# Adaptive-norm attention followed by a GRU: projections split around the transposes, and a last attention batch reordered by pairs of heads

## The chip, the cores and the metric

The kernel runs on one core of one Trainium2 chip. The metric is the device time of one execution in microseconds (us), the median of several executions on one chip. Five engines are spoken of by their profile names: PE (TensorE; its weight loads are listed apart as PEld), DVE (VectorE), ACT (ScalarE), POOL (GpSimd) and SP, whose queue issues nearly all DMAs. All arithmetic is float32.

## The reference

Sixteen sequences (B = 16) of T = 256 tokens with D = 512 features go through an attention block and then a GRU, each with a residual.

```python
# attention, 16 heads of 32
xn  = rms_norm(x, g_norm) * (1 + scale) + shift      # scale, shift from cond @ W_emb + b_emb
q, k, v = split(xn @ W_qkv)
q, k = rms_norm(q, g_q), rms_norm(k, g_k)            # per head
o   = softmax(q @ k.T * 32 ** -0.5) @ v
x   = x + o + o @ W_out
# GRU over the 256 tokens, all 16 sequences at once, state h (16 x 512), h0 = cond
for t in range(256):
    gi, gh = x[:, t] @ W_ih + b_ih, h @ W_hh + b_hh
    r, z = sigmoid(gi_r + gh_r), sigmoid(gi_z + gh_z)
    n = tanh(gi_n + r * gh_n)
    h = (1 - z) * n + z * h
    out[:, t] = x[:, t] + h
```

## The kernel before

The program has two parts: attention, batch by batch, up to about 620 us, and the GRU, step by step, after that. Within each part the order on PE, DVE, ACT and POOL is the order in which the program text issues the instructions; nothing is reordered later. Only SP's DMAs are placed by the framework.

**Attention.** A batch has 16 heads, taken as four groups of four. For a group, `logits` (line 302) multiplies q by k into four PSUM banks `lg0` to `lg3`, one for each head; the contraction is over 32 features, so the four heads use four bands of 32 rows of the array. `maxima` (L326, DVE) takes the negated row maxima, `exps` (L330, ACT) the exponentials with their row sums, `normalize` (L340: a reciprocal on DVE, eight scalings on POOL) divides. In the next group's time the normalised weights are transposed on PE (`turn`, in two halves by `turn_pair`, L350), copied from PSUM into `attnT` (`put_turned_bank`, L371, two banks by DVE and two by ACT), multiplied with v (`weigh`, L383), and the result is copied to `oT` (`put_weighed`, L399).

One group is one slot. PE's spare places in the slots of batch b are filled with the projections of batch b + 1: `project` (L238) adds, for each chunk `k` of 128 features, four matmuls (j = 0 to 3) of 128 x 32 weights against 512 columns. The four write four bands of 32 PSUM partitions, that is four bands of 32 columns of the array. `slot0` to `slot3` (L418 to L538) write out by hand what goes where:

- slot 0: eight chunk steps of `project` for q and k, with `turn_x` (transposes of x) and the turn of the previous group among them;
- slots 1 and 2: five chunk steps ahead of the turn and one behind it, then `weigh`;
- slot 3: four ahead, then the transposes of q and k of one half (`turn_qk`), the turn, `turn_qk` of the other half, two chunk steps, `weigh`.

In slot 3 `turn_qk` needs the normalised q and k that DVE makes in `norm_qk` (L269).

Fifteen batches go through these slots. The sixteenth has no next batch to project; `last_batch` (L586) takes its four groups alone. There a loop pass transposes the previous group in two halves, runs the maxima and exponentials of the current one, copies the transposed banks, and issues the logits of the next group for all four heads; `weigh` of a group comes a pass later. Behind the loop stand the four parts of `project_first` (L545: output projection of the first 16 tokens, 32 matmul records each), the work on the last group, and `open_gates` (L567), which writes the biases into the PSUM banks of the first gates.

**GRU.** W_hh is loaded into `whh`, in the same SBUF place as `wq`, once the last projection has read that. Step 0 begins with three `state_part` calls on the initial state, `h0P`, one for each gate (L881), then `input_part` for two steps. The first instruction of the recurrence proper is the DVE transpose `trr` of gate r (L831).

Of the kernel before, what the change touches and what calls it, by code (L numbers as in the profile page):

```python
# [8 lines left out]
F32 = mybir.dt.float32  # L9
AF = mybir.ActivationFunctionType  # L10
ALU = mybir.AluOpType
AX = mybir.AxisListType
PSUM = bass.MemoryType.PSUM

P = 128
# [4 lines left out]
def kernel(  # L20
# [214 lines left out]
            else:  # L235
                nc.vector.tensor_scalar(dst, tps[r][:, c], a, s, ALU.mult, ALU.add)  # L236

    def project(b, n, s, ks, a):  # L238

        if isinstance(a, str):  # L240
            a = tile_ps(f"qkv_{b}_{n}_{s}", a)
        for k in ks:
            for j in range(4):
                nc.tensor.matmul(  # L244
                    a[32 * j : 32 * j + 32, :],
                    batches[b].xnT[:, k, n * P + 32 * j : n * P + 32 * j + 32],
                    wq[:, k, s * D : (s + 1) * D],
                    start=(k == 0),
                    stop=(k == KC - 1),
                )  # L250
        return a
# [47 lines left out]
    class Group:  # L299
        pass  # L300

    def logits(b, g):

        w = Group()
        w.b, w.g = b, g
        w.lg = [
            ps_lg.tile([P, NT, T], F32, tag=f"lg{i}", name=f"lg_{b}_{g}_{i}") for i in range(HG)
        ]
        for n in range(NT):
            for i in range(HG):  # L310
                r = slice(i * DH, (i + 1) * DH)
                nc.tensor.matmul(  # L312
                    w.lg[i][:, n, :],
                    qT[r, g, n * P : (n + 1) * P],
                    kT[r, g, :],
                    start=True,
                    stop=True,
                )
        w.turned = []
        w.neg = small.tile([P, HG, NT], F32, tag="neg", name=f"neg_{b}_{g}")  # L320
        w.den = small.tile([P, HG, NT], F32, tag="den", name=f"den_{b}_{g}")
        w.rden = small.tile([P, HG, NT], F32, tag="rden", name=f"rden_{b}_{g}")
        w.attn = [None] * HG
        return w

    def maxima(w, heads):  # L326
        for i in heads:
# [131 lines left out]
    def slot1(b, w, prev, st):  # L459
        m = b + 1  # L460
        project(m, 0, 1, (2, 3), st.k)
        st.q1 = project(m, 1, 0, (0, 1, 2), "Z")
        maxima(w, range(HG))
        exps(w, range(HG))
        sq = st.s0.square(1, st.k)
        turn(prev)
        put_turned(prev, "vava")
        project(m, 1, 0, (3,), st.q1)
        st.s0.add(1, sq)
        if b + 3 < B:  # L470
            norm_first(b + 3, (0,))
        st.s0.rs.first()
        st.s1 = Stats(m, 1)
        st.sq = st.s1.square(0, st.q1)
        weigh(prev, "Y")
        put_weighed(prev)
        st.rstd = st.s0.rs.second()
        normalize(w)

    def slot2(b, w, prev, st):  # L480
        m = b + 1
        k = project(m, 1, 1, range(KC), "Y")
        maxima(w, range(HG))
        st.qk0 = norm_qk(m, 0, (st.q, st.k), st.rstd)
        st.v0 = project(m, 0, 2, (0,), "A")
        exps(w, range(HG))
        st.s1.add(0, st.sq)
        sq = st.s1.square(1, k)
        turn(prev)
        put_turned(prev, "vava")  # L490
        project(m, 0, 2, (1,), st.v0)
        st.s1.add(1, sq)
        if b + 3 < B:
            norm_first(b + 3, (1,))
        st.s1.rs.first()
        if b + 3 < B:
            batches[b + 3].rs.first()
        weigh(prev, "X")
        put_weighed(prev)
        if b == 0:  # L500

            for c in range(KC):
                d = wo[:, c, c * P : (c + 1) * P]
                nc.vector.tensor_tensor(d, d, ident, ALU.add)
            load_small()
        elif b == 2:
            for i in range(2):
                a = b_rows[:, 2 * i, :]
                nc.vector.tensor_tensor(a, a, b_more[:, i, :], ALU.add)
        st.accs = (st.q1, k)  # L510
        st.rstd = st.s1.rs.second()
        normalize(w)

    def slot3(b, w, prev, st):
        m = b + 1
        project(m, 0, 2, (2, 3), st.v0)
        st.v1 = project(m, 1, 2, (0, 1), "X")
        maxima(w, range(HG))
        qk1 = norm_qk(m, 1, st.accs, st.rstd)
        tq0 = turn_qk(m, 0, st.qk0, "ZY")  # L520
        if b + 3 < B:
            rstd = batches[b + 3].rs.second()
        exps(w, range(HG))
        put_qk(0, 0, tq0, nc.vector)
        put_qk(0, 1, tq0, nc.scalar)
        put_v(m, 0, st.v0)
        turn(prev)
        put_turned(prev, "vava")
        tq1 = turn_qk(m, 1, qk1, "ZY")
        project(m, 1, 2, (2, 3), st.v1)  # L530
        put_qk(1, 0, tq1, nc.vector)
        put_qk(1, 1, tq1, nc.scalar)
        if b + 3 < B:
            norm_apply(b + 3, rstd)
        normalize(w)
        weigh(prev, "A")
        put_weighed(prev)
        if m == B - 1:  # L538
            put_v(m, 1, st.v1)
# [27 lines left out]
    def open_gates(p, which=(R_, N_, Z_)):  # L567

        for g, name, bank, row, n in (
# [6 lines left out]
            for j in range(4):  # L576
# [6 lines left out]
                    skip_group_check=True,  # L583
                )

    def last_batch(prev):  # L586


        b, before = B - 1, None
        w = logits(b, 0)  # L590
        for g in range(NG):
            if before:
                weigh(before, "Z")
            turn_pair(prev, 0, "AX")
            maxima(w, (0, 1))
            exps(w, (0, 1))
            if before:
                put_weighed(before, nc.vector)
            turn_pair(prev, 1, "YZ")
            maxima(w, (2, 3))  # L600
            exps(w, (2, 3))
            put_turned_bank(prev, 0, nc.vector)
            normalize(w, (0, 1))
            put_turned_bank(prev, 2, nc.vector)
            put_turned_bank(prev, 1, nc.scalar)
            put_turned_bank(prev, 3, nc.scalar)
            if g < NG - 1:
                normalize(w, (2, 3))
                before, prev, w = prev, w, logits(b, g + 1)
        project_first(0)  # L610
        project_first(1)
        normalize(w, (2,), nc.vector)
        normalize(w, (3,))
        turn_pair(w, 0, ("lg2", "lg3"))
        turn_pair(w, 1, "AX")
        weigh(prev, "Z")
        put_turned(w, "vava")
        put_weighed(prev)
        open_gates(0, (R_, N_))
        weigh(w, "Y")  # L620
        put_weighed(w, nc.vector)
        open_gates(0, (Z_,))
        project_first(2)
        project_first(3)

    E = mybir.EngineType
    E = mybir.EngineType
    ORDERED = {E.PE, E.DVE, E.Activation, E.Pool}
    with tc.manual_schedule(engines=ORDERED):
# [5 lines left out]

        pe = tile_ps("ps_emb", "Z", (P, 8 * 32))
        nc.vector.memset(pe, 0.0)

        warm = tile_ps("warm", "Y", (P, P))
        for i in range(12):  # L640
            nc.tensor.matmul(warm, ident, ident, start=True, stop=True)
        tp = tile_ps("tp_h0", "X", (P, KC, B))
        nc.tensor.transpose(
            tp.rearrange("p k b -> p (k b)"), cond_sb, ident[: KC * B, : KC * B]
# [72 lines left out]
        for b in range(B - 1):  # L717
            for g in range(NG):
                w = logits(b, g)
                (slot0, slot1, slot2, slot3)[g](b, w, prev, st)  # L720
                prev = w
        last_batch(prev)

    TG = P // B
    xins = {}

    def in_blocks(a, i, j, s):

        a = a[:, i * TG : (i + 1) * TG, :].rearrange("b (s i) (j f) -> s j b i f", s=2, f=P)
        return a[s, j]

    def load_block(i):
        if i < T // TG:
            xins[i] = xin.tile([P, TG // 2, KC, 32], F32, tag="xin", name=f"xin_{i}")
            for j in range(4):
                for s in range(2):
                    r = 32 * j + B * s
                    nc.sync.dma_start(  # L740
                        xins[i][r : r + B].rearrange("b i q c -> b i (q c)"), in_blocks(x, i, j, s)
                    )

    for i in range(4):
        load_block(i)


    whh = wpool.tile([P, KC, 3 * D], F32, tag="w_b", name="whh")
    load_rows(whh, w_hh)

    work.close()

# [49 lines left out]
        nc.scalar.copy(gates[N_, p % 2][:, 0, :], b_rows[:, 3, :])  # L802
        nc.scalar.copy(gates[Z_, p % 2][:, 0, :], b_rows[:, 2, :])

    def gate_part(dst, rows, w, first, k, stationary):

        for j in range(4):
            nc.tensor.matmul(  # L808
                dst[32 * j : 32 * j + rows],
                stationary,  # L810
                w[:, k, :].rearrange("p (g j c) -> p j g c", g=3, c=P)[:, j, first::2][:, : dst.shape[1]],
                start=False,
                stop=True,
                skip_group_check=True,
            )

    def input_part(p, g, k):

        grp, ti = divmod(2 * p, TI)
        x2 = xTs[grp][:, k, ti : ti + 2, :].rearrange("p t b -> p (t b)")  # L820
        gate_part(gates[g, p % 2], 32, wih, g, k, x2)

    def state_part(t, g, hT):

        for k in range(KC):
            gate_part(gates[g, t // 2 % 2][:, 0:1, :], hT.shape[2], whh, g, k, hT[:, k, :])

    def turned(name, t, gate):

# [39 lines left out]
    with tc.manual_schedule(engines=ORDERED):  # L869
# [7 lines left out]
        for c in (slice(0, 2 * B), slice(2 * B, TI * B)):  # L877
            for i, o in enumerate(first):
                a = xTs[0][:, 2 * i : 2 * i + 2].rearrange("p q t b -> p q (t b)")[:, :, c]
                nc.vector.tensor_tensor(a, o[:, :, c], a, ALU.add)  # L880
        for g in (R_, N_, Z_):  # L881
            state_part(0, g, h0P)

        parts = [(g, k) for g in (R_, Z_) for k in range(KC)]
        for g, k in parts:
# [104 lines left out]
```

## Time and profile before

| what | value |
|---|---|
| time before, median of 3 runs | 1746.63 us (1745.31 to 1748.65) |
| profiled execution, its own time | 1746.58 us |
| span of its trace, first to last instruction | 1744.8 us |
| granted TensorE clock, mean over the span | 0.994 |
| PE busy | 1728.0 us, 99% of the span |
| DVE, ACT, POOL busy | 60%, 42%, 18% of the span |
| first slot of the last batch (its first logits) | 584.22 us |
| first `trr` of the GRU | 625.64 us |

Lines such as L391 are lines of the kernel. In a timeline each row has the start in us, the length, the engine, the line, the operation, what is written from what is read, the shapes and the number of instructions merged in the row. A float32 matmul is two records. The length of a PE row reaches to the modelled end of its last matmul, which overlaps the next row; the time that a block takes of PE is therefore read from the start of its row to the start of the next one.

### The profile page before, as it was taken

To read this page: it belongs to the slowest core of one execution; us is meant where nothing else is said; L and a number is where in the kernel's file an instruction comes from. 1 tells how busy PE (TensorE), PEld (TensorE's weight loads), DVE (VectorE), ACT (ScalarE), POOL (GpSimd) and SP (SyncE) were. 2 spreads that over 40 slices of the span, in tenths; PEclk is the share of its full clock that TensorE was granted. 3 is DMA by queue.
4 is the path that set the end of the run, shared out by engine and by line. 5 is a ranking of instruction groups with operands and counts; after the bars stand their busy time and mean duration, and the time that the engine had idled before them with its cause. 6 is when DMAs were issued, how large, how long until landed. Compare 5 with 4: busy or idle time off the path is not lost.

```text
span 1744.8 us, 95656 instructions
## 1 busy us (share of the span) xinstructions
PE 1728.0 (99%) x42866; PEld 1272.0 (73%) x42866; DVE 1051.4 (60%) x3312; ACT 740.3 (42%) x2694; POOL 315.5 (18%) x773
## 2 busy tenths in 40 slices
PE   8999999999999999999999999999999999999998
PEld 4444444444444589888888888888888888888886
DVE  4777777777776645555555555555555555555554
ACT  4777777777777722222222222222222222222222
POOL 0443344334433410000000000000000000000000
PEclk9999999999999899999999999999999999999999
DMA  9100000000000310000000000000000000000000
GB/s 281 46 14 14 14 26 14 14 14 14 14 2 2 74 28 22 16 17 22 23 16 16 23 22 17 16 22 23 16 16 22 23 16 17 16 10 11 10 17 15
DMA packets 50506, 44.37 MB, mean 25 GB/s; under 512 B 10195, under 2 KB 43327, under 8 KB 50095
## 3 DMA queue, kind: packets, MB, share of 16 engines
q1 hardware_dynamic: 49959, 38.21, 8.3%
q8 instruction: 336, 5.51, 1.3%
q14 instruction: 75, 0.61, 0.1%
q10 hardware_dynamic: 136, 0.04, 0.0%
HBM read 29.79 MB, written 8.39 MB: 22 GB/s over the span
## 4 chain that ended last, share of the span: by engine, by line
PE 95%; DVE 2%; ACT 1%; issue 1%; DMA 0%; POOL 0%; SPq 0%; DVEq 0%; ACTq 0%
PE gr L808 25%; PE qkv L244 19%; PE gz L808 18%; PE gn L808 13%; PE o L765 6%; PE lg L312 4%; PE tpa L218 4%; PE o L391 4%; PE tpqk L218 1%; ACT attn L334 1%; PE tpx L218 0%; PE first L550 0%; DVE trh L831 0%; DMA we<-in_L_cond_W_emb_dram 0%; ACT n L912 0%
## 5 line engine op out<-in xcount | busy, mean ns | idle before, releaser
L244 PE MATMUL qkv<-wq,xnT 128*32 128x512 f32 x3072 | 354.7, 596 | 1.1 <-DVE xnT L236 1.1
L345 POOL TENSOR_SCALAR attn<-attn,rden 128x256 f32<-128x256 f32 x510 | 232.8, 478 | 379.0 <-DVE rden L342 275.2
L906 ACT ACTIVATE r<-trr 128x64 f32<-128x64 f32 x256 | 65.4, 256 | 514.8 <-DVE trr L831 512.8
L808 PE MATMUL gr<-wih,xT 128*32 128x256 f32 x4096 | 268.4, 379 | 0.0
L334 ACT ACTIVATE attn<-lg,neg 128x256 f32<-128x256 f32 x512 | 234.4, 483 | 66.6 <-DVE neg L328 42.6
L831 DVE STREAM_TRANSPOSE trr<-gr 128x128 f32<-128x128 f32 x256 | 81.1, 317 | 274.6 <-PE gr L808 274.6
L244 PEld LDWEIGHTS qkv<-wq,xnT 128*32 128x32 f32 x3072 | 88.3, 109 | 182.1 <-issue 157.2
L912 ACT ACTIVATE n<-n 128x64 f32<-128x64 f32 x256 | 65.6, 256 | 308.6 <-DVE n L911 305.6
L808 PEld LDWEIGHTS gr<-wih,xT 128*32 128x32 f32 x4096 | 135.4, 110 | 82.3
L328 DVE TENSOR_REDUCE neg<-lg 128x2 f32<-128x512 f32 x256 | 159.2, 683 | 48.4 <-PE lg L312 48.2
L831 DVE STREAM_TRANSPOSE trh<-gn 128x128 f32<-128x128 f32 x256 | 81.1, 317 | 116.9 <-PE gn L808 116.9
L765 PE MATMUL o<-oT,wo 128*32 128x256 f32 x1920 | 147.8, 379 | 0.0
L808 PE MATMUL gr<-whh,padded 128*32 128x128 f32 x4096 | 135.9, 273 | 2.9 <-DVE padded L940 1.7
L942 POOL TENSOR_TENSOR y<-xT,padded 128x64 f32<-128x64 f32 x128 | 41.0, 320 | 535.3 <-DVE padded L940 535.3
L808 PEld LDWEIGHTS gr<-whh,padded 128*32 128x32 f32 x4096 | 115.0, 110 | 30.3 <-DVE padded L940 29.4
L808 PE MATMUL gz<-wih,xT 128*32 128x128 f32 x4096 | 135.5, 273 | 0.0
L808 PE MATMUL gz<-whh,padded 128*32 128x128 f32 x4096 | 135.5, 273 | 0.0
L808 PE MATMUL gn<-whh,padded 128*32 128x128 f32 x4096 | 135.5, 273 | 0.0
L808 PE MATMUL gr<-whh,h 128*16 128x128 f32 x4064 | 134.6, 273 | 0.4
L808 PE MATMUL gn<-whh,h 128*16 128x128 f32 x4064 | 134.5, 273 | 0.0
L808 PE MATMUL gz<-whh,h 128*16 128x128 f32 x4064 | 134.4, 273 | 0.0
L808 PEld LDWEIGHTS gz<-wih,xT 128*32 128x32 f32 x4096 | 117.8, 110 | 21.2
(119 smaller groups left out, 2499.8 us busy)
## 6 DMA issues: line engine op xcount, KB each, us to landing
x<-in_x_dram SPq DMA_DIRECT2D x16, 512.0 KB, 3.6
xin<-in_x_dram SPq DMA_DIRECT2D x256, 32.0 KB, 1.9
out_dram<-osb SPq DMA_DIRECT2D x248, 32.0 KB, 1.8
wq<-in_L_cond_W_qkv_dram SPq DMA_DIRECT2D x4, 768.0 KB
wih<-in_L_cond_W_ih_dram SPq DMA_DIRECT2D x16, 192.0 KB, 6.9
whh<-in_L_cond_W_hh_dram SPq DMA_DIRECT2D x16, 192.0 KB, 6.4
we<-in_L_cond_W_emb_dram SPq DMA_DIRECT2D x4, 512.0 KB, 4.9
wo<-in_L_cond_W_out_dram SPq DMA_DIRECT2D x1, 1024.0 KB, 17.8
```

The lines of the kernel that those rows point to most:

```text
L218: nc.tensor.transpose(dst[r], src[q], ident[q, q])
L244: nc.tensor.matmul(a[32 * j : 32 * j + 32, :], batches[b].xnT[:, k, n * P + 32 * j : n * P + 32 * j + 32], wq[:, k, s * D : (s + 1) * D], ...
L312: nc.tensor.matmul(w.lg[i][:, n, :], qT[r, g, n * P : (n + 1) * P], kT[r, g, :], start=True, stop=True,)
L328: nc.vector.tensor_reduce(w.neg[:, i, :], w.lg[i], AX.X, ALU.max, negate=True)
L334: nc.scalar.activation(a[:, n, :], w.lg[i][:, n, :], AF.Exp, bias=w.neg[:, i, n : n + 1], accum_out=w.den[:, i, n : n + 1],)
L345: engine.tensor_scalar(w.attn[i][:, n, :], w.attn[i][:, n, :], w.rden[:, i, n : n + 1], 1.0, ALU.mult, ALU.mult,)
L391: nc.tensor.matmul(w.o[i * DH : (i + 1) * DH, :], v[:, k, h * DH : (h + 1) * DH], w.attnT[:, i, k, :], start=(k == 0), stop=(k == NT - 1),)
L765: nc.tensor.matmul(acc[32 * j : 32 * j + 32, :], w[:, k, P * j + 32 * m : P * j + 32 * m + 32], rhs, start=(k == 0), stop=(k == KC - 1),)
L808: nc.tensor.matmul(dst[32 * j : 32 * j + rows], stationary, w[:, k, :].rearrange("p (g j c) -> p j g c", g=3, c=P)[:, j, first::2][:, : ds ...
L831: nc.vector.transpose(tr.rearrange("p q s b -> p (q s b)"), gate)
L906: nc.scalar.activation(r, turned("r", t, gr[:, 0, :])[:, :, s, :], AF.Sigmoid)
L912: nc.scalar.activation(n, n, AF.Tanh)
```

## The change

- `project` takes a list of column bands `js`. In slot 1 the chunk k = 2 of q, and in slot 2 the chunk k = 0 of v, is split: bands 0, 1 and 2 stay where the whole chunk was, ahead of the turn, and band 3 goes behind the turn, ahead of the chunk that was there already.
- In slot 3 the whole chunk k = 2 of the second v projection moves from behind the transposes to ahead of them.
- `logits` can be issued for some heads; `add_logits` issues the others.
- `last_batch` works by pairs of heads: all four maxima of the current group are taken before the pass begins, the logits and maxima of the next group come in two pairs, and `weigh` follows in the same pass as the transposes. `keep_busy` issues four products of the identity with itself, 128 x 128, at two places of a pass; nothing reads their result. The parts of `project_first` are dealt among the last steps.
- The three `state_part` calls of step 0 move into `last_batch`. The first four loads of x for the GRU and the load of `whh` are issued by the program ahead of `last_batch`.

```diff
-    def project(b, n, s, ks, a):
+    def project(b, n, s, ks, a, js=range(4)):
...
-            for j in range(4):
+            for j in js:
...
+    def add_logits(w, heads):
+        for i in heads:
+            w.lg[i] = ps_lg.tile([P, NT, T], F32, tag=f"lg{i}", name=f"lg_{w.b}_{w.g}_{i}")
+        for n in range(NT):
+            for i in heads:
...
     def slot1(b, w, prev, st):
...
-        st.q1 = project(m, 1, 0, (0, 1, 2), "Z")
+        st.q1 = project(m, 1, 0, (0, 1), "Z")
+        project(m, 1, 0, (2,), st.q1, (0, 1, 2))
...
         put_turned(prev, "vava")
+        project(m, 1, 0, (2,), st.q1, (3,))
         project(m, 1, 0, (3,), st.q1)
...
     def slot2(b, w, prev, st):
...
-        st.v0 = project(m, 0, 2, (0,), "A")
+        st.v0 = project(m, 0, 2, (0,), "A", (0, 1, 2))
...
         put_turned(prev, "vava")
+        project(m, 0, 2, (0,), st.v0, (3,))
         project(m, 0, 2, (1,), st.v0)
...
     def slot3(b, w, prev, st):
...
-        st.v1 = project(m, 1, 2, (0, 1), "X")
+        st.v1 = project(m, 1, 2, (0, 1, 2), "X")
...
-        project(m, 1, 2, (2, 3), st.v1)
+        project(m, 1, 2, (3,), st.v1)
...
+    def keep_busy(bank, n):
+        warm = tile_ps("warm", bank, (P, P))
+        for i in range(n):
+            nc.tensor.matmul(warm, ident, ident, start=True, stop=True)
+
     def last_batch(prev):
-        b, before = B - 1, None
-        w = logits(b, 0)
+        w = logits(B - 1, 0)
+        maxima(w, range(HG))
         for g in range(NG):
-            if before:
-                weigh(before, "Z")
+            last = g == NG - 1
             turn_pair(prev, 0, "AX")
-            maxima(w, (0, 1))
             exps(w, (0, 1))
-            if before:
-                put_weighed(before, nc.vector)
+            put_turned_bank(prev, 0, nc.vector)
+            keep_busy("Y", 4)
             turn_pair(prev, 1, "YZ")
-            maxima(w, (2, 3))
-            exps(w, (2, 3))
-            put_turned_bank(prev, 0, nc.vector)
+            put_turned_bank(prev, 2, nc.vector)
             normalize(w, (0, 1))
-            put_turned_bank(prev, 2, nc.vector)
             put_turned_bank(prev, 1, nc.scalar)
             put_turned_bank(prev, 3, nc.scalar)
-            if g < NG - 1:
-                normalize(w, (2, 3))
-                before, prev, w = prev, w, logits(b, g + 1)
-        project_first(0)
+            if last:
+                project_first(0)
+            else:
+                after = logits(B - 1, g + 1, (0, 1))
+                maxima(after, (0, 1))
+            weigh(prev, "Y")
+            exps(w, (2, 3))
+            put_weighed(prev, nc.vector)
+            if last:
+                break
+            normalize(w, (2, 3))
+            keep_busy("A", 4)
+            add_logits(after, (2, 3))
+            maxima(after, (2, 3))
+            prev, w = w, after
         project_first(1)
         normalize(w, (2,), nc.vector)
         normalize(w, (3,))
-        turn_pair(w, 0, ("lg2", "lg3"))
-        turn_pair(w, 1, "AX")
-        weigh(prev, "Z")
-        put_turned(w, "vava")
-        put_weighed(prev)
+        turn_pair(w, 0, "AX")
+        put_turned_bank(w, 0, nc.vector)
+        put_turned_bank(w, 1, nc.scalar)
+        project_first(2)
+        turn_pair(w, 1, "YZ")
+        put_turned_bank(w, 2, nc.vector)
+        put_turned_bank(w, 3, nc.scalar)
         open_gates(0, (R_, N_))
-        weigh(w, "Y")
+        weigh(w, "A")
         put_weighed(w, nc.vector)
         open_gates(0, (Z_,))
-        project_first(2)
+        state_part(0, R_, h0P)
         project_first(3)
+        state_part(0, N_, h0P)
+        state_part(0, Z_, h0P)
...
+        for i in range(4):
+            load_block(i)
+        whh = wpool.tile([P, KC, 3 * D], F32, tag="w_b", name="whh")
+        load_rows(whh, w_hh)
         last_batch(prev)
...
-        for g in (R_, N_, Z_):
-            state_part(0, g, h0P)
```

More of the change, by code (lines that the diff above doesn't have):

```diff
@@ L300, with logits @@
         pass
-    def logits(b, g):
+    def logits(b, g, heads=range(HG)):
         w = Group()
         w.b, w.g = b, g
[L306 to L318, printed above, removed]
+        w.lg = [None] * HG
+        if heads:
+            add_logits(w, heads)
         w.turned = []
@@ L324, in logits @@
         return w
+    def add_logits(w, heads):
[3 more added lines that the diff above has]
+            for i in heads:
+                r = slice(i * DH, (i + 1) * DH)
+                nc.tensor.matmul(
+                    w.lg[i][:, n, :],
+                    qT[r, w.g, n * P : (n + 1) * P],
+                    kT[r, w.g, :],
+                    start=True,
+                    stop=True,
+                )
     def maxima(w, heads):
@@ L584, in open_gates, with gate_part, state_part @@
                 )
+    def gate_part(dst, rows, w, first, k, stationary):
+        for j in range(4):
+            nc.tensor.matmul(
+                dst[32 * j : 32 * j + rows],
+                stationary,
+                w[:, k, :].rearrange("p (g j c) -> p j g c", g=3, c=P)[:, j, first::2][:, : dst.shape[1]],
+                start=False,
+                stop=True,
+                skip_group_check=True,
+            )
+    def state_part(t, g, hT):
+        for k in range(KC):
+            gate_part(gates[g, t // 2 % 2][:, 0:1, :], hT.shape[2], whh, g, k, hT[:, k, :])
@@ new lines, with in_blocks, load_block @@
+    TG = P // B
+    xins = {}
+    def in_blocks(a, i, j, s):
+        a = a[:, i * TG : (i + 1) * TG, :].rearrange("b (s i) (j f) -> s j b i f", s=2, f=P)
+        return a[s, j]
+    def load_block(i):
+        if i < T // TG:
+            xins[i] = xin.tile([P, TG // 2, KC, 32], F32, tag="xin", name=f"xin_{i}")
+            for j in range(4):
+                for s in range(2):
+                    r = 32 * j + B * s
+                    nc.sync.dma_start(
+                        xins[i][r : r + B].rearrange("b i q c -> b i (q c)"), in_blocks(x, i, j, s)
+                    )
@@ L637 @@
         nc.vector.memset(pe, 0.0)
-        warm = tile_ps("warm", "Y", (P, P))
-        for i in range(12):
-            nc.tensor.matmul(warm, ident, ident, start=True, stop=True)
+        keep_busy("Y", 12)
         tp = tile_ps("tp_h0", "X", (P, KC, B))
@@ L721 @@
                 prev = w
+        for i in range(4):
+            load_block(i)
+        whh = wpool.tile([P, KC, 3 * D], F32, tag="w_b", name="whh")
+        load_rows(whh, w_hh)
         last_batch(prev)
[L726 to L749, printed above, removed]
     work.close()
@@ L803, in seed @@
         nc.scalar.copy(gates[Z_, p % 2][:, 0, :], b_rows[:, 2, :])
[L805 to L815, printed above, removed]
     def input_part(p, g, k):
@@ L821, in input_part @@
         gate_part(gates[g, p % 2], 32, wih, g, k, x2)
-    def state_part(t, g, hT):
-        for k in range(KC):
-            gate_part(gates[g, t // 2 % 2][:, 0:1, :], hT.shape[2], whh, g, k, hT[:, k, :])
     def turned(name, t, gate):
```

## The prediction

> **What bounds the kernel now.** I read the page first, for the bound.
>
> ```profile
> PE 1728.0 (99%) x42866; PEld 1272.0 (73%) x42866; DVE 1051.4 (60%) x3312; ACT 740.3 (42%) x2694; POOL 315.5 (18%) x773
> PE 95%; DVE 2%; ACT 1%; issue 1%; DMA 0%; POOL 0%; SPq 0%; DVEq 0%; ACTq 0%
> ```
>
> PE is 95% of the chain that ended last. No engine can become cheaper to any effect except PE, and a microsecond added to PE's order in the attention part is a microsecond of time. Next come PE's own rows in slots 0, 1 and 2 of one batch, in the timeline. Starts matter here, not lengths.
>
> ```profile
> 517.42 1.93 PE L244 MATMUL qkv<-wq,xnT 128*32 128x512 f32 x16
> 519.16 1.05 PE L391 MATMUL o<-attnT,v 128*32 128x256 f32 x16
> 520.14 1.15 PE L312 MATMUL lg<-kT,qT 32*128 32x256 f32 x16
> 521.22 4.50 PE L244 MATMUL qkv<-wq,xnT 128*32 128x512 f32 x40
> 525.64 1.21 PE L218 MATMUL tpa<-ident,attn 64*128 64x64 f32 x32
> 526.78 1.07 PE L244 MATMUL qkv<-wq,xnT 128*32 128x512 f32 x8
> 527.67 1.27 PE L391 MATMUL o<-attnT,v 128*32 128x256 f32 x16
> 528.87 1.15 PE L312 MATMUL lg<-kT,qT 32*128 32x256 f32 x16
> 535.53 1.07 PE L244 MATMUL qkv<-wq,xnT 128*32 128x512 f32 x8
> 536.41 1.21 PE L391 MATMUL o<-attnT,v 128*32 128x256 f32 x16
> 537.56 0.71 PE L312 MATMUL lg<-kT,qT 32*128 32x256 f32 x8
> ```
>
> One chunk of a projection (8 records) takes 0.88 (526.78 to 527.67), two take 1.74 (517.42 to 519.16). `weigh` takes 0.98 in slot 0, 1.20 in slot 1 and 1.15 in slot 2: there it waits 0.22 and 0.17 for the copies into `attnT`, since only one chunk lies between turn and `weigh`. These waits, and one in slot 3, are what the moves can take away.
>
> ```profile
> 515.68 0.71 PE L218 MATMUL tpx<-ident,xs 64*128 64x64 f32 x16
> 542.21 0.96 PE L218 MATMUL tpqk<-ident,qkn 64*128 64x64 f32 x16
> 542.94 1.22 PE L218 MATMUL tpa<-ident,attn 64*128 64x64 f32 x32
> ```
>
> Sixteen transposes of x take 0.55 (515.68 to the turn at 516.23); the same number of q and k take 0.73 in slot 3, where they wait for `norm_qk`. Last, the last batch: its timeline and its windows.
>
> ```profile
> 587.24 0.69 PE L312 MATMUL lg<-kT,qT 32*128 32x256 f32 x2 [0.40 <-ACT attn L334]
> 598.64 1.94 PE L391 MATMUL o<-attnT,v 128*32 128x256 f32 x16
> 600.51 1.97 PE L218 MATMUL tpa<-ident,attn 64*128 64x64 f32 x32
> 605.85 1.93 PE L391 MATMUL o<-attnT,v 128*32 128x256 f32 x16
> ...
> 584.20:591.40 7.20, 6.16 (x68) 3.65 (x64) 4.59 (x10) 5.74 (x20) 5.01 (x12) 0.94 0.99 234
> 591.40:598.60 7.20, 7.20 (x65) 4.56 (x64) 4.44 (x11) 4.82 (x18) 3.58 (x8) 0.50 0.90 204
> 598.60:605.80 7.20, 7.20 (x65) 4.56 (x64) 4.42 (x11) 4.82 (x18) 3.64 (x9) 0.50 0.01 3
> ```
>
> A pass is 7.21 (598.64 to 605.85), at a granted clock of 0.50, where `weigh` takes 1.87 instead of 0.98. The first row is one head's logits matmul alone on its quarter of the array: 0.69, no less than a head takes beside three others.
>
> **Slots 1 and 2: the split chunk.** PE only; no DMA and nothing on SP or POOL moves. The tempting price of a fourth of a chunk is 0.22, exactly the wait. But the four bands of a chunk run at the same time; the 0.88 is the time of any one of them. Ahead of the turn, bands 0 to 2 alone still take 0.88, so the turn starts when it did. Behind the turn, band 3 has two chunks to do, one after the other, while bands 0 to 2 have one; then `weigh` uses the same four bands, and the next logits use all columns and need band 3 finished. So the stretch from the end of the turn to the next logits is set by band 3: two chunks and `weigh`, which is slot 0's row, 517.42 to 520.14 = 2.72. Now it is 526.78 to 528.87 = 2.09 in slot 1, 535.53 to 537.56 = 2.03 in slot 2. Cost 0.63 + 0.69 = 1.32 a batch, the removed waits already in it; 15 batches: **+19.8**. The trace shows no band of 32 columns alone, so bounds: with a fourth at a fourth of the price, -0.22 - 0.17 a batch (-5.9); with the whole chunk, +19.8. The nearest row, the lone 0.69 of a row band, shows no discount, and I take the upper end. The Trainium skill, TensorEngine Tiling (Array Packing), Key Properties, says that tiles operate independently, but that changing the tiling mode drains TensorE. By its first half alone, `weigh` on bands 0 to 2 would cover the quarter and the cost would be nothing; the second half brings the wait back at the logits, which have another mode. The row at 528.87, where the logits follow the last `weigh` record, fits the second half.
>
> **Slot 3.** One whole chunk moves ahead of the first `turn_qk`: 0.88 more before it and less after it, no extra. The first `turn_qk` starts at about 543.07 instead of 542.21. DVE's `norm_qk` ends at about 542.4, so the wait goes: 0.73 to 0.55, -0.18. What is late next is `weigh`, with one chunk less ahead of it: turn, copies and the second `turn_qk` shift by about 0.65 together, ACT's last `attnT` copy to about 546.15, and `weigh` would start at 546.45. Cover 0.3; if it were gone, a wait as in slot 1 (0.2) would return and cancel the gain. 15 x -0.18 = **-2.7** (bounds -4 and +0.5).
>
> **Last batch.** Its bound after the change must be found by adding PE's order of a pass at full clock: two turn halves 1.24 (1.14 for a turn in slot 1, and one more change of mode), `weigh` 0.98, logits in two pairs. A pair is no cheaper than four heads (1.08, slot 0), since the heads run side by side: 2.15, of which 1.08 is new. The eight products: in the first microseconds 24 records of this product came 0.21 apart; `state_part` at full clock, 128 columns too, has bursts 0.11 apart. Four products are 0.9 or 1.7; I take 0.95 with the change of mode, as the rest of the batch would be at full clock; 1.9 a pass. Sum 6.3, with small waits 6.4. The other chain of a pass (second pair's exponentials, reciprocal, four scalings 1.8 on POOL, turn half, ACT copy, exponentials) gives 5.6, and DVE and ACT 4.4 and 4.8. So PE is the bound at 6.4 against 7.21, and the products are no longer filling a wait but on the path.
>
> I laid the orders side by side. Pass 0 ends no earlier: four maxima (to 587.9) now stand ahead of the two copies on DVE, `weigh` waits for the second one to about 589.4, and the second turn half of pass 1 comes at about 594.2, as now. Two passes at 6.4 instead of 7.21 bring that of pass 3 to 606.9, against 608.6 now. From there PE is full: two more turn halves and this one 1.7, four parts of `project_first` 7.0, two `weigh` 2.0, biases 1.4, three `state_part` 2.6, `input_part` up to the first `trr` 2.0: 16.7, so `trr` at 623.6 against 625.64: **-2.0**. `put_weighed` now stands ahead of the second reciprocal on DVE, and behind it the scalings on POOL; it ends 0.15 after the exponentials do, in the 6.4. In pass 3 it also holds back head 2's scaling, which has `project_first(1)` as cover. The 16 loads of `whh` and the x loads are issued earlier in the text, but SP already issues `whh` from 583.49 to 592.3, with 6.4 to landing; the first `state_part` comes at about 617, so their cost is nothing with 18 of cover.
>
> Here the page TensorE: Matmul & The Clock Gate, Terms, has a rule: the penalty of a throttled stretch is its length times (1 - K/N). The clock is 0.50 from 590.6 to 607.6, 17 us, so 8.5 would be saved if the products hold it up. The rows say otherwise: laid out at full clock, the old order would reach `trr` 4.3 earlier, since a pass then waits for ACT and DVE for 5.8; the split logits and the products spend some 2 of these. By the rule the sum would be 1755; I take the rows. If the clock falls in spite of the products, PE's 6.3 doubles in two passes or more, and the batch is some 6.7 slower than now.
>
> **Sum.** The profiled execution took 1746.58, 1.8 around its span; the median is 1746.63, so the sum serves for both. 1746.6 + 19.8 - 2.7 - 2.0 = **1761.7**.
>
> **The rivals.**
> - *A fourth costs a fourth (faster).* If lone bands were cheap, or their work hid beside the transposes, the two waits go: -5.9 - 2.7 - 2.0 = 1736. For it: 1.74 for eight matmuls reads as 0.22 each, and waits of that size are there. Against: the lone 0.69 row, and transposes that need all columns. It decides from the point at which band 3's second chunk costs less than 0.25 a slot. 13%.
> - *Half of it hides*: one of band 3's two passes (0.43) beside something else, 30 slots: 1749. No row for it. 4%.
> - *The clock falls in the last batch*: 1761.7 + 8.7 = 1770. For it: transposes and pair logits leave the array part empty. 8%.
> - *As summed*: 75%, with 1757 to 1766 of its own (slot 3 from -4 to +0.5, products up to the price of the first microseconds).
>
> Low 1748 and high 1770 leave out the first rival and little else. About 0.2% is what a measurement of this kernel can tell from no change. Faster 0.13, same 0.02, slower 0.85.
>
> **What would show it.** Right: in slots 1 and 2, turn to next logits 2.7 instead of 2.0 to 2.1, no wait of L391 for ACT; a batch of 37.7 instead of 36.56; `tpqk` at 0.55; passes of about 6.4 at clock 1.00. Wrong: turn to logits of 1.9, or a batch of 36.2 or less; or passes still over 7 at clock 0.50.

## The result and the profile after

The changed kernel takes 1762.02 us (median of 5 runs, 1761.56 to 1762.77) against 1745.31 (5 runs, 1743.48 to 1748.65) for the kernel before on the same chip: 1.0094 times as long, 95% interval 1.0082 to 1.0106. The profiled execution took 1762.77, with a span of 1761.0. The granted TensorE clock differs between executions of one program, between 8 and 21 us and in the last batch; the comparisons below say where that matters.

The page of the changed kernel shows no new bound. PE's busy time has grown by 16.6 us, the span by 16.2. DMA's 2% of the chain lies in the first 33 us, where the chain runs over two loads; the first logits come only 1.13 later than before.

```profile
PE 1744.6 (99%) x42922; PEld 1286.4 (73%) x42922; DVE 1052.3 (60%) x3313; ACT 745.4 (42%) x2693; POOL 317.2 (18%) x773
PE 94%; DVE 2%; DMA 2%; ACT 1%; issue 1%; POOL 0%; SPq 0%; DVEq 0%; ACTq 0%
```

Cutting both spans at the same rows of the timelines gives the balance. The rows are the first logits of slot 1 in batch 0, the first logits of the last batch, the first `trr` of the GRU and the end.

| stretch | before, us | after, us | difference |
|---|---|---|---|
| up to slot 1 of batch 0 | 44.09 | 45.22 | +1.13 |
| slots of batches 0 to 14 | 540.13 | 556.23 | +16.10 |
| last batch, up to the first `trr` | 41.42 | 40.28 | -1.14 |
| GRU | 1119.15 | 1119.25 | +0.10 |

The first row is no part of the change: in this execution the clock was at half for 3.4 us during the first projections, in the profiled one of before it was not. The rest is in the slots. PE's timeline there, slot 1 of batch 13 from its logits to those of slot 2; the lines of the kernel have moved, so `weigh` is L395 and the logits are L322:

```profile
535.19 1.15 PE L322 MATMUL lg<-kT,qT 32*128 32x256 f32 x16
536.27 4.49 PE L244 MATMUL qkv<-wq,xnT 128*32 128x512 f32 x38
540.69 1.21 PE L218 MATMUL tpa<-ident,attn 64*128 64x64 f32 x32
541.83 1.47 PE L244 MATMUL qkv<-wq,xnT 128*32 128x512 f32 x9
542.72 0.80 PE L395 MATMUL o<-attnT,v 128*32 128x256 f32 x6
543.14 0.59 PE L244 MATMUL qkv<-wq,xnT 128*32 128x512 f32 x1
543.15 1.45 PE L395 MATMUL o<-attnT,v 128*32 128x256 f32 x10
544.53 1.15 PE L322 MATMUL lg<-kT,qT 32*128 32x256 f32 x16
```

Read the record counts. Ahead of the turn stand 38 records instead of 40, but they last 4.42 (536.27 to 540.69), as long as 40 records did (521.22 to 525.64): leaving band 3 out saved nothing. Behind the turn, 10 records belong to projections, two for band 3's first chunk and eight for the second chunk. The last of them, band 3's second record of the second chunk, starts alone at 543.14, when `weigh` has already begun on the other bands at 542.72. So `weigh` no longer waits for ACT, as intended: the trace of before has 31 waits of its weight loads for ACT's copies, 9.8 us in all, this one has 3, of 1.0 us. But the next logits come 2.70 after the turn (541.83 to 544.53) instead of 2.09. They follow the last record of `weigh`, and that one comes late, because band 3's share of `weigh` begins only after its second chunk. A narrow window shows the last record of `weigh` alone, here and, below the dots, in slot 1 of before:

```profile
544.22 0.38 PE L395 MATMUL o<-attnT,v 128*32 128x256 f32 x1
...
528.56 0.38 PE L391 MATMUL o<-attnT,v 128*32 128x256 f32 x1
```

From it to the logits it is 0.31 in both kernels (544.22 to 544.53, 528.56 to 528.87). So nothing new is paid at the logits themselves; what has moved is the end of the fullest band.

In slot 3 the transposes of q and k no longer wait:

```profile
521.71 0.72 PE L218 MATMUL tpqk<-ident,qkn 64*128 64x64 f32 x16
522.26 1.16 PE L218 MATMUL tpa<-ident,attn 64*128 64x64 f32 x32
...
524.21 1.06 PE L244 MATMUL qkv<-wq,xnT 128*32 128x512 f32 x8
525.09 1.05 PE L395 MATMUL o<-attnT,v 128*32 128x256 f32 x16
526.07 1.15 PE L322 MATMUL lg<-kT,qT 32*128 32x256 f32 x16
```

They take 0.55 (521.71 to 522.26) instead of 0.73, and `weigh` keeps its 0.98: the one chunk behind the turn covers its copies.

A pass of the last batch, from one block of products (`warm`) to the same block of the next pass, and two windows of about a pass each, in which the clock is the third number from the end:

```profile
614.25 1.16 PE L634 MATMUL warm<-ident 128*128 128x128 f32 x8
615.33 1.13 PE L322 MATMUL lg<-kT,qT 32*128 32x256 f32 x8
616.40 0.71 PE L218 MATMUL tpa<-ident,attn 64*128 64x64 f32 x16
617.04 1.16 PE L634 MATMUL warm<-ident 128*128 128x128 f32 x8
618.35 0.71 PE L218 MATMUL tpa<-ident,attn 64*128 64x64 f32 x16
...
621.05 1.16 PE L634 MATMUL warm<-ident 128*128 128x128 f32 x8
...
608.40:615.20 6.80, 6.65 (x82) 4.89 (x81) 4.46 (x9) 5.05 (x21) 3.69 (x8) 1.00 1.03 225
615.20:622.10 6.90, 6.75 (x82) 4.91 (x81) 4.46 (x9) 4.93 (x19) 3.69 (x8) 1.00 0.04 9
```

The clock is at 1.00 throughout. A pass is 6.80 (614.25 to 621.05); two blocks of four products take 1.08 and 1.31 of it. The second, ahead of a half turn, takes 0.23 more than the first, ahead of logits; no run here shows why.

### The profile page after: what moved, and what is told of

Its sections match the earlier page's. It is cut to its first block, busy times and chain, and to the rows that moved or that the text cites. A ratio compares the mean times of both kernels' runs of the same rounds, so it can differ in the third digit from the quotient of the medians.

```text
span 1761.0 us, 95774 instructions
## 1 busy us (share of the span) xinstructions
PE 1744.6 (99%) x42922; PEld 1286.4 (73%) x42922; DVE 1052.3 (60%) x3313; ACT 745.4 (42%) x2693; POOL 317.2 (18%) x773
## 4 chain that ended last, share of the span: by engine, by line
PE 94%; DVE 2%; DMA 2%; ACT 1%; issue 1%; POOL 0%; SPq 0%; DVEq 0%; ACTq 0%
PE gr L596 25%; PE qkv L244 19%; PE gz L596 18%; PE gn L596 13%; PE o L800 6%; PE o L395 4%; PE lg L322 4%; PE tpa L218 4%; PE tpqk L218 1%; DMA wih<-in_L_cond_W_ih_dram 1%; PE tpx L218 0%; PE first L557 0%; ACT attn L338 0%; PE warm L634 0%; DMA we<-in_L_cond_W_emb_dram 0%
## 5 line engine op out<-in xcount | busy, mean ns | idle before, releaser
L244 PE MATMUL qkv<-wq,xnT 128*32 128x512 f32 x3072 | 381.2, 598 | 1.1 <-DVE xnT L236 1.1
L244 PEld LDWEIGHTS qkv<-wq,xnT 128*32 128x32 f32 x3072 | 93.9, 110 | 201.9 <-issue 177.2
```

Source lines behind the costliest of these rows:

```text
L244: nc.tensor.matmul(a[32 * j : 32 * j + 32, :], batches[b].xnT[:, k, n * P + 32 * j : n * P + 32 * j + 32], wq[:, k, s * D : (s + 1) * D], ...
```

## Experiments

**Is it the split, and nothing else?** The kernel before with the split alone:

```diff
-        st.q1 = project(m, 1, 0, (0, 1, 2), "Z")
+        st.q1 = project(m, 1, 0, (0, 1), "Z")
+        project(m, 1, 0, (2,), st.q1, (0, 1, 2))
...
+        project(m, 1, 0, (2,), st.q1, (3,))
         project(m, 1, 0, (3,), st.q1)
...
-        st.v0 = project(m, 0, 2, (0,), "A")
+        st.v0 = project(m, 0, 2, (0,), "A", (0, 1, 2))
...
+        project(m, 0, 2, (0,), st.v0, (3,))
         project(m, 0, 2, (1,), st.v0)
```

> The kernel before with only the two split chunks of slots 1 and 2 (bands 0 to 2 ahead of the turn, band 3 behind it). Theory band (band 3 has two chunks in a row behind the turn and the next logits wait for it): a batch of 37.8 us instead of 36.56, turn to next logits 2.7 in both slots, about 19 us slower than before, near 1764.5. Rival quarter (a fourth of a chunk costs 0.22 and fills the wait): 6 us faster, near 1740. Rival elsewhere (the slowdown of the changed kernel comes from slot 3 or from the last batch): no change here.

Measured: 1764.70 (4 runs), 1.0115 times before (1.0097 to 1.0134). The slots of batches 0 to 14 take 559.08 against 540.13, +18.95, or 1.26 a batch. From turn to next logits it is 2.70 in slots 1 and 2 of all fifteen batches. The rival in which a fourth costs a fourth is out, and the one that looks elsewhere too.

**The reverse**, the changed kernel with whole chunks:

```diff
-        st.q1 = project(m, 1, 0, (0, 1), "Z")
-        project(m, 1, 0, (2,), st.q1, (0, 1, 2))
+        st.q1 = project(m, 1, 0, (0, 1, 2), "Z")
...
-        project(m, 1, 0, (2,), st.q1, (3,))
...
-        st.v0 = project(m, 0, 2, (0,), "A", (0, 1, 2))
+        st.v0 = project(m, 0, 2, (0,), "A")
...
-        project(m, 0, 2, (0,), st.v0, (3,))
```

> The changed kernel with whole chunks again in slots 1 and 2, everything else kept. Theory band: the 19 us go, and what is left of the change (slot 3, -0.18 a batch, and the last batch, -1) shows: about 1742.5, 3 to 4 us faster than before. Rival quarter or elsewhere: still 1756 or more.

Measured: 1744.66 (12 runs), ratio 0.9994 (0.9985 to 1.0002). The slots take 537.17, 2.96 less than before. The slowdown is gone. But 3 to 4 us of gain were expected and the interval allows 2.6 at most: this expectation was missed. What the profiles say of the rest stands with the last batch below.

**Is it the cut, or the uneven load?** Here the two chunks are cut in the same places, but ahead of the turn band 3 does its part of the other chunk, so that each side has four bands of equal load:

```diff
-        st.q1 = project(m, 1, 0, (0, 1, 2), "Z")
+        st.q1 = project(m, 1, 0, (0, 1), "Z")
+        project(m, 1, 0, (2,), st.q1, (0, 1, 2))
+        project(m, 1, 0, (3,), st.q1, (3,), last=2)
...
-        project(m, 1, 0, (3,), st.q1)
+        project(m, 1, 0, (3,), st.q1, (0, 1, 2))
+        project(m, 1, 0, (2,), st.q1, (3,), last=2)
```

(slot 2 likewise; `first` and `last` name the chunks that open and close a band's sum.)

> The kernel before with the chunks split in both slots, but with even load: ahead of the turn bands 0 to 2 of one chunk and band 3 of the other, behind it the rest. Same number of matmuls on each side as before, two chunks cut apart. Theory band: each band has the same load on both sides, so turn to next logits stays at 2.0 to 2.1 and the time within 2 us of before. Rival cut (cutting a chunk apart is dear in itself, by more weight loads that aren't prefetched or by changes of mode): 10 us slower or more.

Measured: 1746.40 (20 runs), ratio 1.0005 (0.9998 to 1.0012); the slots take 540.15 against 540.13. PE's timeline in slots 1 and 2 is that of before; slot 1:

```profile
527.11 1.06 PE L244 MATMUL qkv<-wq,xnT 128*32 128x512 f32 x8
527.99 1.27 PE L391 MATMUL o<-attnT,v 128*32 128x256 f32 x16
529.19 1.15 PE L312 MATMUL lg<-kT,qT 32*128 32x256 f32 x16
```

From turn to logits 2.08. Cutting these chunks apart is free; leaving a band idle on one side of a turn is not.

**Does the cost go with the number of matmuls moved?** The same split, two bands and two; the diff is against the split alone, and slot 2 is likewise:

```diff
-        project(m, 1, 0, (2,), st.q1, (0, 1, 2))
+        project(m, 1, 0, (2,), st.q1, (0, 1))
...
-        project(m, 1, 0, (2,), st.q1, (3,))
+        project(m, 1, 0, (2,), st.q1, (2, 3))
```

> The kernel before with the chunks split two and two: bands 0 and 1 ahead of the turn, bands 2 and 3 behind it. Theory band: the same as for three and one, since both sides last as long as one band's chunk: turn to next logits 2.7, a batch of 37.8, near 1764.5. Rival count (the cost goes with the number of matmuls behind the turn): twice the price of three and one, or with the quarter's price a gain and then a wait less than in three and one: a batch of 36.2 or of 39.

Measured: one run, 1765.15; the slots take 559.13, within 0.1 of the 559.08 with one band moved.

```profile
546.81 1.48 PE L244 MATMUL qkv<-wq,xnT 128*32 128x512 f32 x10
547.70 0.60 PE L391 MATMUL o<-attnT,v 128*32 128x256 f32 x4
548.12 0.60 PE L244 MATMUL qkv<-wq,xnT 128*32 128x512 f32 x2
548.13 1.45 PE L391 MATMUL o<-attnT,v 128*32 128x256 f32 x12
549.51 1.15 PE L312 MATMUL lg<-kT,qT 32*128 32x256 f32 x16
```

Now two projection records trail `weigh` at 548.12 instead of one, and the logits still come 2.70 after the turn. The price is that of the fullest band; a second band as full adds nothing.

**Slot 3 alone:**

```diff
-        st.v1 = project(m, 1, 2, (0, 1), "X")
+        st.v1 = project(m, 1, 2, (0, 1, 2), "X")
...
-        project(m, 1, 2, (2, 3), st.v1)
+        project(m, 1, 2, (3,), st.v1)
```

> The kernel before with only the whole chunk moved in slot 3. Theory (the first transposes of q and k no longer wait for DVE): tpqk from 0.73 to 0.55, a batch of 36.43 instead of 36.62, no new wait of weigh, 2.8 us faster: about 1742.5. Rival given back (the chunk that is gone behind the turn uncovers a wait of weigh there): a batch of 36.6, time as before.

Measured: 1742.96 (22 runs), ratio 0.9984 (0.9977 to 0.9992); the slots take 537.40, -2.73. This part of the change is a gain and nothing takes it back.

**The products of the identity: filling or path?** The changed kernel with whole chunks (no_split), and eight products instead of four at each place:

```diff
-            keep_busy("Y", 4)
+            keep_busy("Y", 8)
...
-            keep_busy("A", 4)
+            keep_busy("A", 8)
```

> The changed kernel with whole chunks in slots 1 and 2 and eight products instead of four at each of the seven places. Theory price: PE sets the pass, so each call's further 0.86 us is paid in full: the stretch from 40.3 to about 46, a pass from 6.8 to 8.5. Rival filling (the products lie where PE waits): the stretch stays within 1 us.

Measured: one run, 1752.79; the stretch to `trr` grows from 40.27 to 46.41, that is 6.14 for seven places, 0.88 each.

```profile
600.65 2.05 PE L631 MATMUL warm<-ident 128*128 128x128 f32 x16
...
609.24 2.05 PE L631 MATMUL warm<-ident 128*128 128x128 f32 x16
```

A pass is 8.59 (600.65 to 609.24) instead of 6.80: each product added to the four is paid in full.

**Without them** (the diff is against no_split):

```diff
-            keep_busy("Y", 4)
...
-            keep_busy("A", 4)
```

> The changed kernel with whole chunks in slots 1 and 2 and without the products of the identity in the last batch; the step from no_split is the products alone. Theory price (the products are on PE's path and the clock would mostly hold without them): from the last batch's first logits to the first trr 38 to 39 us instead of 40.3, with passes under 6. Rival clock (without the products the clock falls to 0.50): that stretch 42 to 47, slower than no_split by 2 us or more.

Measured: 1746.30 (22 runs), ratio 0.9993 (0.9981 to 1.0006), and each of the two theories holds for a part of the executions. Eight of the 22 took 1738.1 to 1740.1 with a mean clock of 0.998 or more, fourteen took 1745.7 to 1751.1 with 0.989 to 0.993, and none lies between. The profile shows one of the eight: clock at 1.00, a pass of 5.32, a stretch of 35.79, 4.5 less than with the products and below the 38 to 39 expected. None of the fourteen was profiled: their means show that the clock fell, not where. No execution with four products (12 of no_split, 5 of the changed kernel) has a mean clock below 0.997. So the products do hold the clock, and cost about half of what its fall costs: 4.5 against 9.3 between the medians of the two sets.

**Half as many** (against no_split):

```diff
-            keep_busy("Y", 4)
+            keep_busy("Y", 2)
...
-            keep_busy("A", 4)
+            keep_busy("A", 2)
```

> The changed kernel with whole chunks in slots 1 and 2 and two products of the identity at each place instead of four. Without products a pass of the new order took 5.3 us, of which PE waits about 1.0; four products at two places took 6.8. Theory: two at each place (about 0.55 with the changes of mode) fill the wait, so a pass is 5.3 to 5.8 and the stretch to the first trr 36 to 37.5; the clock holds in most executions or in all: 1739 to 1741. Rival: two are too few and the clock falls in part of the executions, which then take 1745 or more.

Measured: 1742.38 (5 runs, 1740.16 to 1743.33), ratio 0.9967 (0.9954 to 0.9979). The stretch was 37.70, at a clock of 1.00, and no run reached 1745. But time and stretch lie above the 1739 to 1741 and 36 to 37.5 expected: two products do not fit into the wait without cost. In the stretch, the first two products at seven places cost 1.91 (35.79 to 37.70), the next two 2.57 (to 40.27), and each further two 3.07 (to 46.41 for eight). The fewer there are, the more of them lies in waits.

**Products where PE waits.** The order of before, with slot 3's move (not shown again), and six products behind the second half turn, into the bank of the head whose exponentials are done first:

```diff
             turn_pair(prev, 1, "YZ")
+            if g < NG - 1:
+                warm = tile_ps("warm", "lg0", (P, P))
+                for i in range(6):
+                    nc.tensor.matmul(warm, ident, ident, start=True, stop=True)
```

> The kernel before with slot 3's move and, in its own last batch, six products of the identity behind the second turn half of each of the first three passes, into the bank of the first head, where PE waits about 2 us for ACT. Theory: the clock stays at 1.00 and the products cost nothing there, so the stretch is about 37 us (against 41.4, 39.6, 38.4 and 37.4 seen in the old order with 17, 10, 7 and 3 us at half clock): 1740 to 1741, faster than both kernels. Rival: the products are late and delay the next logits, or the clock falls all the same: 39 or more.

Measured: 1740.77 (9 runs), ratio 0.9973 (0.9963 to 0.9983); the stretch 36.67 with the clock at 1.00.

```profile
593.55 1.60 PE L603 MATMUL warm<-ident 128*128 128x128 f32 x12
...
598.97 1.60 PE L603 MATMUL warm<-ident 128*128 128x128 f32 x12
```

A pass is 5.42 (593.55 to 598.97), six products in it, against 7.21 at half clock without them. This beats both kernels without the new order of the last batch. The new order without products has a stretch of 35.79, also at 1.00: at equal clock the order by pairs is worth at most about 0.9 us.

**And at the start.** The same with products in the waits of the first 13 us (only these are shown):

```diff
             for j in range(4):
                 nc.tensor.matmul(
                     pe[32 * j : 32 * j + B, :],
...
+            if k < KC - 1:
+                for i in range(2):
+                    nc.tensor.matmul(warm, ident, ident, start=True, stop=True)
...
         tpx = turn_x(0, ("lg0", "lg1"))
+        for i in range(4):
+            nc.tensor.matmul(warm, ident, ident, start=True, stop=True)
```

> old_order_products with products of the identity also in the first 13 us: two behind each of the first three chunks of the embedding matmul, where PE waits 0.5 to 0.7 us for a DMA, and four ahead of the first projection, where it waits 1.1 us for DVE. In the profiles so far the first projections ran at half clock for 0 to 10 us, and the first logits came at 33.5 to 37.4. Theory: the products keep the clock up there, first logits at 33.5 to 34.0, 1738 to 1739.5. Rival: the half clock there comes for another reason, or the products delay the embedding: first logits at 35 or later, 1741 or more.

Measured: 1739.29 (5 runs, 1738.75 to 1739.80), ratio 0.9951 (0.9938 to 0.9965): the lowest ratio here, though its interval touches that of the version above. First logits at 33.83.

## Why the prediction was right, point by point

- *Slots 1 and 2: +19.8, band 3 sets the end.* Shown. The split alone costs 18.95 in the slots, even load makes it free, and two bands cost what one does. The size is 1.26 a batch instead of 1.32: the stretch was taken from slot 0's row (2.72; slot 0 has six chunk steps, four ahead of the turn and two behind it) and measured 2.70, and each turn starts 0.01 earlier. The prediction leans on the Trainium skill, TensorEngine Tiling (Array Packing), Key Properties, by which a change of tiling mode drains TensorE. The trace agrees: `weigh` runs on the other bands beside band 3's last projection record (542.72 against 543.14), and the logits, in another mode, come 0.31 behind the start of its last record. But it does not show that the mode is the reason. The logits write all 128 columns (`32*128` in their rows), band 3's among them, so they would have to wait for band 3 without any drain, as the prediction itself says a few lines earlier. Its remark that independent tiles alone would make the cost nothing does not follow. No run here separates the two.
- *Slot 3: -2.7.* Shown: -2.73 alone, with the transposes at 0.55 in all fifteen batches. The cover for `weigh` held.
- *Last batch: -2.0.* It measured -1.14 against the profiled execution of before. The mis-sized term is the four products, 0.95 in the sum: a block takes 1.08 to 1.31, so a pass is 6.80 and not 6.4, which is 0.8 over the two passes of the sum. That the products lie on PE's path was right, as doubling them shows; but taking them out gains only 1.48 a pass (6.80 to 5.32), since PE then waits for other engines.
- *What the prediction did not see* is that this term was reckoned against one draw of the clock. Five profiles have the old order without products: the stretch took 41.42 with 17.1 us at half clock (before), 39.55 with 10.2 (split_only), 38.36 with 6.8 (balanced), 37.44 and 37.43 with 3.4 (split_22, slot3_only). The changed order takes 40.28 and 40.27 in its two profiles with four products. Against four of the five it is no gain. This fits no_split (0.9994) lying behind slot3_only (0.9984), but their intervals overlap, so it is not shown by the times.
- *The clock's rule.* The Trainium skill, TensorE: Matmul & The Clock Gate, Terms, puts the penalty at length x (1 - K/N), K/N being the granted share of the clock: 8.5 us for the 17 us. The five profiles give about 0.3 us for each microsecond at half clock (37.43 at 3.4 to 41.42 at 17.1, 3.99 over 13.7), not 0.5, so taking the rows was right. With no half clock in the stretch, the old order took 36.67, 4.75 less than 41.42, with 18 products in its waits (old_order_products); the prediction had 4.3. The other executions agree, as an estimate from each one's time and mean clock: a straight line through the 47 runs of before beside no_products gives 0.33 us per microsecond at half clock, and one through the 22 of no_products gives 0.33 too. By this estimate the two sets there lie 9.3 apart because more time is spent at half clock, not because a microsecond of it costs more.
- *The rivals.* The quarter at a quarter's price is excluded, and so is the half that hides: 2.70 leaves no room for 0.43 less. In the six profiles with products in the last batch the clock did not fall there; without products it fell in 14 of 22 executions, by their mean clocks.
- *The sum* hit 1762.02 with 1761.7 partly by luck. The slots cost 1.0 less than forecast (16.10 for 17.1), the last batch gained 0.9 less, and 1.1 came from the start of the execution that was profiled. As a difference, 15.1 was forecast and 16.7 measured (1762.02 less 1745.31).

## What to carry to other kernels

In this kernel, a group of matmuls that share the array by column bands cost what its fullest band cost. Dividing the group's time by its count gives a price at which nothing is sold: moving one of four saved nothing where it was taken away and cost a whole group where it was put, unless another band's work went the other way. Work that only keeps the clock up belongs in PE's measured waits; beyond what the waits hold it is path, and doubling it shows which it is. And before a stretch is compared with a forecast, look at its clock in more than one profile.

## What the runs showed of the hardware

- Whether the clock falls can differ from execution to execution: one and the same program (no_products) held it in 8 executions and lost it in 14, with 5.6 us between the two sets. A single profile of such a stretch tells neither its typical nor its worst time.
- The first projections also run at half clock for 0 to 10 us, by execution, and the first logits come later with it: in the twelve profiles at 33.5 to 33.8 with none, 34.4 to 35.0 with 3.4 us, 35.6 to 36.3 with 6.8 and 37.1 to 37.4 with 10.2. Four profiles without the products that start_too adds there had none either, so its one profile proves nothing. Its five runs all have a mean clock of 0.999 or 1.000, against five of nine of old_order_products; that fits the products' holding the clock there, but is too few to show it.
- The recorded clock misses a slow start: in no_split the 24 records of the identity product that open the program come 0.21 apart at first and 0.11 apart from the sixteenth on, while the clock is recorded as 1.00 from 1.3 to 5.7 us. In before they stay 0.21 apart, at 1.00 too.
- Bands run ahead of each other across instructions: records of `weigh` started 0.42 before the last record of a projection that stands earlier in the program (542.72 against 543.14).
